# A graph network of GRU and attention layers on one core: more transposes through the DMA crossbar, and GpSimd broadcasts of f_j

## The chip, the core and the metric

The kernel runs on one core of one Trainium2 chip. The metric is the time of one execution on the device in microseconds, as the median of several runs. The core has TensorE (PE, matmuls and transposes, results to PSUM), ScalarE (ACT), VectorE (DVE), GpSimd (POOL) and SyncE (SP), which here only issues DMAs. Each engine takes its instructions in the order in which they were written and waits on semaphores for the others.

## The reference

There are 128 graphs of 128 nodes with 256 features, and an integer adjacency matrix for each. All is float32.

```python
# layer 0: three steps of a gated graph network
A = (adj != 0); h = x
for i in range(3):
    m = h @ weight[i]
    aggr = einsum('bst,bsd->btd', A, m)
    h = gru_cell(aggr, h, w_ih, w_hh, b_ih, b_hh)     # r, z: sigmoid; n: tanh
x = layernorm(x + h)
# layers 1 to 3: graph attention, each with its own W and a
Wh = x @ W.T
f_i, f_j = Wh @ a1, Wh @ a2
e = leaky_relu(f_i[:, :, None] + f_j[:, None, :], 0.2)
e = where(adj == 0, very_negative, e)
x = layernorm(x + softmax(e, axis=2) @ Wh)            # layer 2: rows without a neighbour give 0
```

## The kernel before

The 128 graphs are taken four at a time (`G = 4`), so there are 32 groups (`NG`). For each group `gru` (L516) does the three steps of layer 0 and `gat` (L648) the three attention layers.

In a step of `gru` the nodes' features are needed in two layouts. `hT` has the features on the partitions and four graphs of 128 nodes along the free dimension (two tiles for the 256 features, `KC = 2`). It feeds the gate products (L490), which `strassen` (L473) arranges as seven block products instead of eight, with sums and differences of blocks made by `sums` (L450, L460). `h` has the nodes on the partitions; it is the stationary operand of the aggregation by the mask `am` (L548). After steps one and two the new `hT2` has to be turned into `h`; after step three it has to be turned once more to be added to the input `y` (L635).

There are two ways to turn a tile. TensorE transposes four 128x128 blocks into a PSUM bank (L632 and others), and ScalarE or VectorE copies the bank out. `turned` (L375) goes through the DMA crossbar, which transposes 16-bit elements: one copy parts a float32 tile into its low and high halves (L382), SP issues the DMA transpose (L383), and a second copy joins the halves (L386). Before the change the crossbar is used for `x` of the groups from the third on and for `h` of steps one and two in all but the last four groups.

In a layer of `gat`, VectorE forms f_i and f_j as products with a row of `wa` and a sum (L660), one column for each graph. TensorE then transposes the column of f_j, broadcast along the free dimension, so that every partition gets the row of f_j in PSUM (L673, four transposes). VectorE adds the mask and takes the maximum (L678). ScalarE applies the leaky slope (L682) and the exponential with its sum (L699). TensorE transposes the scores (L706), which are copied out (for the first layer by `EVICT`; for the others with the scale of the previous layer norm, L711 or L715) and multiplied with the features (L736) and the weights (L747). VectorE adds the residual (L753); the sums of squares come from ScalarE (L434), epsilon from GpSimd (L438, and L418 in `layernorm`), and the power -0.5 from GpSimd (L406).

The order in which all this is issued is not written by hand. Every operation is given to a planner (`Plan`, L48) with the engines that may do it, a cost in ns for each, and the tiles that it reads and writes. `Plan.order` runs through time, gives each engine the ready operation with the lowest priority number, and emits the instructions in that order. An operation of TensorE counts as ready only `LATENCY` of the producer's engine and `MARGIN` after its last producer; a DMA has 4000 ns of latency on SP, to which an operation can add a `lag`. Operations marked `BOTH` or run on GpSimd share a port in the plan. Buffers are slots of a few kinds: `k2` (2 KB for each partition), `k4` (4 KB), `am`, PSUM banks `gate` and `bank`; a slot that is not free makes an operation wait in the plan. The priority of an operation comes from `stage` (L765): the number of its group, and for the last four groups (`LAST`) a number that takes them through their steps side by side. So the middle of the run is a steady state in which one group's attention is mixed with the GRU steps of the following ones, and the tail has four groups at once and nothing behind them.

Of the kernel before, what the change touches and what calls it, by code (L numbers as in the profile page):

```python
# [14 lines left out]
P = 128  # L15
# [32 lines left out]
class Plan:  # L48
# [6 lines left out]

    MARGIN = 300
# [8 lines left out]
    def op(self, engines, fn, reads=(), writes=(), prio=0, lag=0, port=("POOL",), start=0):  # L65
        o = Op(engines, fn, (prio[0], len(self.ops)), lag, port)
        o.group = prio[1]
        o.earliest = start
        norm = lambda k: k if isinstance(k, tuple) else (k, 0)
        for k in map(norm, reads):  # L70
            if k in self.writer:
                o.deps.add(self.writer[k])
            self.readers.setdefault(k, []).append(o)
            o.bufs.append(k[0])
        for k in map(norm, writes):
            if k in self.writer:
                o.deps.add(self.writer[k])
            o.deps.update(self.readers.pop(k, ()))
            self.writer[k] = o
            o.bufs.append(k[0])  # L80
        o.deps.discard(o)
        o.bufs = [b for b in dict.fromkeys(o.bufs) if b.tag]
        for b in o.bufs:
            b.left += 1
        self.ops.append(o)
# [113 lines left out]
def adj_resnorm_kernel(  # L199
# [24 lines left out]
    pools = {"gru": 5, "xs": 2, "adj": 2, "am": 4, "k2": 27, "k4": 18, "fx": 2, "jx": 2, "f": 4, "mv": 4, "st": 6, "v": 24,  # L224
             "gate": 4, "bank": 4}
    own = ({"k2": 6, "k4": 5, "gate": 1, "bank": 1, "v": 5, "fx": 0, "jx": 0, "st": 0}, {"k2": 3, "k4": 1, "bank": 1, "v": 5, "fx": 0, "jx": 0, "st": 0})
    floats = {"gru": 0, "k4": 1024, "xs": 1024, "fx": 256, "jx": 256, "f": 8, "mv": 8, "st": 6, "v": 4}
    tags = {t: (n, floats.get(t, 512)) for t, n in pools.items()}
    U16 = mybir.dt.uint16
    BOTH = ("DVE", "POOL")  # L230
    plan = Plan({t: n for t, (n, _) in tags.items()}, own)
    slots = {t: [(psum if t in ("gate", "bank") else work).tile([P, w], I32 if t == "adj" else F32, name=f"{t}{i}")
# [22 lines left out]


    ident = consts.tile([P, P], F32)
    make_identity(nc, ident)
# [35 lines left out]
    APART = {"ACT": 1000, "DVE": 620}  # L294
    TURN = 0
# [79 lines left out]
    def turned(src, key, dst, shape, prio):  # L375


        rows = Buf("k2", GN)
        flat = lambda: T(dst) if shape else T(dst).rearrange("p b q -> p (b q)")
        halves_of = lambda at: at.bitcast(U16).rearrange("p (h b q) -> p h b q", h=2, b=G)  # L380
        pairs_of = lambda at: at.bitcast(U16).rearrange("p b (q h) -> p h b q", h=2)
        plan.op(APART, lambda e: copy(e, halves_of(flat()), pairs_of(src())), reads=[key], writes=[dst], prio=prio, port=BOTH)  # L382
        plan.op({"SP": 1200}, lambda e: nc.sync.dma_start_transpose(  # L383
            T(rows).bitcast(U16).rearrange("p (a q) -> p a q", q=P), flat().bitcast(U16)),
            reads=[dst], writes=[rows], prio=prio, lag=TURN)
        plan.op(APART, lambda e: copy(e, pairs_of(T(dst).rearrange(shape, b=G) if shape else T(dst)), halves_of(T(rows))),  # L386
                reads=[rows], writes=[dst], prio=prio, port=BOTH)

# [21 lines left out]
    def layernorm(y, dst, prio):  # L410
# [7 lines left out]
        plan.op({"POOL": 229}, lambda e: nc.gpsimd.tensor_scalar(T(ve), T(mv)[:, :, 1], EPS, None, op0=ALU.add),  # L418
# [5 lines left out]
        for b in range(G):  # L424
            plan.op({"ACT": 500}, lambda e, b=b: nc.scalar.activation(  # L425
                T(dst)[:, b, :], T(y)[:, b, :], AF.Identity, bias=T(shift)[:, b:b + 1], scale=T(rstd)[:, b:b + 1]),
                reads=[(y, b), shift, rstd], writes=[(dst, b)], prio=prio)

    def deviation(y, before, prio):

        ss, ve = Buf("v", G), Buf("v", G)
        for b in range(G):
            jx = Buf("jx", D)
            plan.op({"ACT": 490}, lambda e, b=b, jx=jx: nc.scalar.activation(  # L434
                T(jx), T(y)[:, b, :], AF.Square, accum_out=T(ss)[:, b:b + 1]),
                reads=[(y, b)], writes=[jx, (ss, b)], prio=prio)
        if before is None:
            plan.op({"POOL": 229}, lambda e: nc.gpsimd.tensor_scalar(  # L438
# [77 lines left out]
    def gru(g, stage):  # L516

        xs, adj_i, am = Buf("xs", G, D), Buf("adj", G, P), Buf("am", G, P)
# [4 lines left out]
        plan.op({"SP": 60}, lambda e: nc.sync.dma_start(T(adj_i), adj[g * G:(g + 1) * G].rearrange("b s t -> s b t")),  # L523
                writes=[adj_i], prio=prio)
        if g == 0:
            input_weights(0, prio)
            hidden_weights(prio)
        plan.op({"DVE": 417}, lambda e: nc.vector.tensor_scalar(T(am), T(adj_i), 0, None, op0=ALU.not_equal),
                reads=[adj_i], writes=[am, turn], prio=prio, port=BOTH)
        if g < 2:  # L530
            hT = transposed(xs, lambda b, c: T(xs)[:, b, c * P:(c + 1) * P], prio)
        else:
            hT = [Buf("k2", GN) for c in range(KC)]
            for c in range(KC):
                turned(lambda c=c: T(xs)[:, :, c * P:(c + 1) * P], xs, hT[c], "p (b q) -> p b q", prio)
        h = None
        for i in range(STEPS):
            prio = stage(g, i)
            if g == 0 and i > 0:
                input_weights(i, prio)  # L540
# [76 lines left out]
            if last:  # L617
                y = Buf("k4", G, D)
                plan.op({"SP": 60}, lambda e: nc.sync.dma_start(T(y), x_g), reads=[agg[0]], writes=[y], prio=prio)
                plan.op({"DVE": 417}, lambda e: nc.vector.tensor_scalar(  # L620
# [3 lines left out]
            for c in range(KC):  # L624
                if not last and g < NG - LAST:
                    turned(lambda c=c, hT2=hT2: T(hT2[c]).rearrange("p (b q) -> p b q", b=G), hT2[c], h2[c], None, prio)
                    continue
# [20 lines left out]
    def gat(g, xc, no, stage):  # L648
# [3 lines left out]
        for l in range(3):  # L652
            prio = stage(g, STEPS + l)
            if g == 0:
                score_weights(l, prio)
            f = Buf("f", G, 2)
            for h in (1, 0):
                for b in range(G):
                    fx = Buf("fx", D)
                    plan.op({"DVE": 345}, lambda e, b=b, h=h, l=l, f=f, fx=fx, xc=xc: nc.vector.scalar_tensor_tensor(  # L660
                        T(fx), T(xc)[:, b, :], 1.0, T(wa)[:, l, h, :], op0=ALU.mult, op1=ALU.mult,
                        accum_out=T(f)[:, b, h:h + 1]), reads=[(xc, b), (wa, l)], writes=[fx, (f, 2 * b + h)], prio=prio, port=BOTH)
                if l:
                    plan.op({"DVE": 100}, lambda e, h=h, f=f, rstd=rstd: nc.vector.tensor_mul(
                        T(f)[:, :, h], T(f)[:, :, h], T(rstd)), reads=[(f, 2 * b + h) for b in range(G)] + [rstd],
# [3 lines left out]
            b_ = bank()  # L669

            def fn(e, b_=b_, f=f):
                for b in range(G):
                    nc.tensor.transpose(T(b_)[:, b * P:(b + 1) * P],  # L673
                                        T(f)[:, b, 1:2].to_broadcast([P, P]), ident)
            plan.op({"PE": 440}, fn, reads=[(f, 2 * b + 1) for b in range(G)], writes=[b_], prio=prio)

            for b in range(G):
                plan.op({"DVE": 215}, lambda e, b_=b_, b=b, e_=e_, top=top: nc.vector.tensor_tensor_reduce(  # L678
                    T(e_)[:, b, :], T(b_)[:, b * P:(b + 1) * P], T(no)[:, b, :], 1.0, 3 * FAR, ALU.add, ALU.max,
                    T(top)[:, b:b + 1]), reads=[b_, no], writes=[(e_, b), (top, b)], prio=prio)  # L680
            for b in range(G):
                plan.op({"ACT": 285}, lambda e, b=b, f=f, e_=e_: nc.scalar.activation(  # L682
                    T(e_)[:, b, :], T(e_)[:, b, :], AF.Prelu, bias=T(f)[:, b, 0:1], alpha=SLOPE),
                    reads=[(f, 2 * b), (e_, b)], writes=[(e_, b)], prio=prio)
            if l == 1:
# [6 lines left out]
                T(top), T(top), -1.0, T(f)[:, :, 0], op0=ALU.mult, op1=ALU.subtract),  # L692
# [9 lines left out]
            b_ = bank()  # L702

            def fn(e, b_=b_, e_=e_):
                for b in range(G):
                    nc.tensor.transpose(T(b_)[:, b * P:(b + 1) * P], T(e_)[:, b, :], ident)  # L706
            plan.op({"PE": 440}, fn, reads=[(e_, b) for b in range(G)], writes=[b_], prio=prio)
            if l:
                def scaled(e, b_=b_, pT=pT, rstd=rstd):
                    if e == "DVE":  # L710
                        nc.vector.tensor_mul(T(pT), T(b_).rearrange("p (b j) -> p b j", b=G),  # L711
                                             T(rstd).unsqueeze(2).to_broadcast([P, G, P]))
                    else:
                        for b in range(G):
                            nc.scalar.mul(T(pT)[:, b, :], T(b_)[:, b * P:(b + 1) * P], T(rstd)[:, b:b + 1])  # L715
                plan.op({"DVE": 630, "ACT": 1100}, scaled, reads=[b_, rstd], writes=[pT], prio=prio)
            else:
                plan.op(EVICT, lambda e, b_=b_, pT=pT: copy(e, T(pT).rearrange("p b j -> p (b j)"), T(b_)),
                        reads=[b_], writes=[pT], prio=prio)
# [45 lines left out]
    def stage(g, n):  # L765

        tail = NG - LAST
        return (g + (0 if n >= STEPS else 0) if g < tail else tail + n), 2 * g + (n >= STEPS)
# [5 lines left out]
    with tc.manual_schedule():  # L774
        for o in order:
# [43 lines left out]
```

## Time and profile before

| what | us |
|---|---|
| median of 3 runs | 2620.24 (2620.14 to 2620.81) |
| profiled execution, its own time | 2620.86 |
| its span, first to last instruction | 2618.9 |
| TensorE busy | 2578.3 |
| VectorE busy | 2084.6 |
| ScalarE busy | 1817.4 |
| GpSimd busy | 535.0 |
| 172 DMA transposes, each from issue to landing | 3.1 (median) |

"Busy" is the time in which at least one instruction of the engine has a record. Matmuls overlap each other on TensorE, so the mean of a group there is longer than the distance from one to the next; that distance is read from the chain of work that ended last, which lists pieces in order of time with their start and their length. In the sums by stage a line has the stretch, its length, then busy time and count for PE, PEld (weight loads), DVE, ACT and POOL, then the granted clock of TensorE, the share of the DMA engines and GB/s. In a line of groups the columns are: line, engine, operation, tiles out<-in with shapes, count, busy us and mean ns of one, and idle time before them with what ended it.

### The profile page before, as it was taken

The numbers are of one execution on the slowest core, as the hardware profiler recorded it, in microseconds if no ns is written. First come the engines' busy times: TensorE is split into PE (matmuls) and PEld (weight loads), VectorE is DVE, ScalarE is ACT, GpSimd is POOL, SyncE is SP. The second block draws the span as 40 slices with busy tenths as digits, with TensorE's granted clock in tenths as the row PEclk, the third lists the DMA queues.
The fourth block names the chain that finished last, engine by engine and source line by source line (L and its number), as shares of the span: only waits on it lengthen the run. The fifth ranks groups of instructions, "written<-read, shape, count | busy, mean of one in ns | idle before, by whom it ended". The sixth has DMA issues, their size and how long they took to land.

```text
span 2618.9 us, 41369 instructions
## 1 busy us (share of the span) xinstructions
PE 2578.3 (98%) x13848; PEld 2297.8 (88%) x13848; DVE 2084.6 (80%) x6162; ACT 1817.4 (69%) x4572; POOL 535.0 (20%) x602
## 2 busy tenths in 40 slices
PE   8999999999999999999999999999999999999988
PEld 7888888888889988888888889888889888888877
DVE  6688878888888888788888888888888878856787
ACT  5677666767777767777777777777777777654566
POOL 2122221212122222122212122212122212211111
PEclk9999999999999999999999999999999999999999
DMA  5211111212112111112211121211122221000000
GB/s 146 52 29 37 47 51 25 53 45 48 36 39 53 45 45 42 36 45 53 45 45 41 33 49 45 53 45 41 33 49 45 50 48 37 21 9 25 9 1 33
DMA packets 251734, 110.43 MB, mean 42 GB/s; under 512 B 184320, under 2 KB 249856, under 8 KB 251520
## 3 DMA queue, kind: packets, MB, share of 16 engines
q1 hardware_dynamic: 251088, 107.77, 17.2%
q8 instruction: 109, 1.79, 0.3%
q14 instruction: 105, 0.86, 0.1%
q10 hardware_dynamic: 432, 0.01, 0.0%
HBM read 45.89 MB, written 16.78 MB: 24 GB/s over the span
## 4 chain that ended last, share of the span: by engine, by line
PE 92%; DVE 6%; ACT 1%; issue 1%; DMA 0%; POOLq 0%; SPq 0%; ACTq 0%; DVEq 0%
PE gate L490 64%; PE bank L747 11%; PE bank L736 6%; PE bank L548 6%; DVE fx L660 1%; PE bank L706 1%; PE bank L673 1%; PE bank L632 1%; DVE k L753 1%; PE bank L341 1%; DVE k L290 1%; DVE k L495 0%; DVE k L610 0%; DVE k L678 0%; DVE k L590 0%
## 5 line engine op out<-in xcount | busy, mean ns | idle before, releaser
L490 PE MATMUL gate<-k,whs 128*128 128x256 f32 x4032 | 1202.8, 380 | 2.6 <-DVE k L495 1.8
L490 PE MATMUL gate<-k,wcs 128*128 128x256 f32 x4032 | 1201.0, 379 | 0.0
L490 PEld LDWEIGHTS gate<-k,wcs 128*128 128x128 f32 x4032 | 767.3, 190 | 104.5
L490 PEld LDWEIGHTS gate<-k,whs 128*128 128x128 f32 x4032 | 734.9, 191 | 88.5 <-DVE k L495 2.5
L495 DVE TENSOR_TENSOR k<-gate,k 128x512 f32<-128x512 f32 x576 | 391.9, 685 | 204.0 <-PE gate L490 143.6
L747 PE MATMUL bank<-gwT,k 128*128 128x256 f32 x1536 | 348.9, 380 | 0.4 <-DVE k L290 0.2
L460 POOL TENSOR_TENSOR k<-k,k 128x256 f32<-128x256 f32 x251 | 214.5, 862 | 557.0 <-DVE k L460 236.3
L747 PEld LDWEIGHTS bank<-gwT,k 128*128 128x128 f32 x1536 | 288.7, 190 | 41.2 <-DVE k L290 2.4
L574 ACT ACTIVATE k<-k,brz 128x256 f32<-128x256 f32 (+1 forms) x384 | 225.1, 621 | 134.8 <-DVE k L495 134.8
L660 DVE SCALAR_TENSOR_TENSOR fx<-k,wa 128x256 f32<-128x256 f32 x768 | 285.6, 424 | 16.4 <-ACT k L425 16.3
L288 ACT COPY k<-k 128x1024 uint16<-128x1024 uint16 x203 | 257.7, 1290 | 10.8 <-DVE k L613 7.8
L288 ACT COPY k<-bank 128x512 f32<-128x512 f32 (+1 forms) x307 | 177.2, 581 | 115.7 <-PE bank L736 48.0
L434 ACT ACTIVATE jx<-k 128x256 f32<-128x256 f32 x384 | 156.0, 407 | 133.8 <-DVE k L753 133.1
L556 ACT COPY k<-gate 128x512 f32<-128x512 f32 x288 | 166.9, 581 | 88.7 <-PE gate L490 88.2
L406 POOL TENSOR_TENSOR v<-v,neghalf 128x4 f32<-128x4 f32 x128 | 134.6, 1051 | 375.8 <-DVE v L445 353.1
L753 DVE SCALAR_TENSOR_TENSOR k<-bank,v,k 128x256 f32<-128x256 f32 x384 | 166.7, 474 | 40.4 <-PE bank L747 40.2
L736 PEld LDWEIGHTS bank<-k,k 128*128 128x128 f32 x1536 | 189.5, 195 | 8.8 <-DVE k L290 1.6
L736 PE MATMUL bank<-k,k 128*128 128x128 f32 x1536 | 190.5, 278 | 3.0 <-DVE k L290 1.2
L699 ACT ACTIVATE k<-k,v 128x128 f32<-128x128 f32 x384 | 149.3, 390 | 61.4 <-DVE v L695 61.3
L603 ACT ACTIVATE k<-k,bi 128x512 f32<-128x512 f32 x192 | 137.6, 718 | 70.7 <-DVE k L600 47.1
L610 DVE SCALAR_TENSOR_TENSOR k<-k,k 128x512 f32<-128x512 f32 x192 | 143.4, 748 | 40.9 <-POOL k L608 39.9
L560 ACT ACTIVATE k<-gate,bhn 128x256 f32<-128x256 f32 x288 | 135.9, 472 | 50.7 <-PE gate L490 47.2
(90 smaller groups left out, 2995.6 us busy)
## 6 DMA issues: line engine op xcount, KB each, us to landing
xs<-in_x_dram SPq DMA_DIRECT2D x32, 512.0 KB, 3.8
k<-in_x_dram SPq DMA_DIRECT2D x32, 512.0 KB, 3.9
out_dram<-k SPq DMA_DIRECT2D x32, 512.0 KB, 2.9
adj<-in_adj_dram SPq DMA_DIRECT2D x32, 256.0 KB, 2.8
k<-k SPq DMA_TRANSPOSE x172, 3.1
k<-in_gnn_wT_dram SPq DMA_DIRECT2D x3, 256.0 KB, 4.8
k<-in_w_ihT_dram SPq DMA_DIRECT2D x2, 384.0 KB, 5.6
k<-in_w_hhT_dram SPq DMA_DIRECT2D x2, 384.0 KB, 6.0
```

The costliest lines, as they stand in the source:

```text
L288: nc.scalar.copy(dst, src)
L434: plan.op({"ACT": 490}, lambda e, b=b, jx=jx: nc.scalar.activation(T(jx), T(y)[:, b, :], AF.Square, accum_out=T(ss)[:, b:b + 1]), reads=[( ...
L460: nc.vector if e == "DVE" else nc.gpsimd).tensor_tensor(T(t)[:, j, :], a(), b(), ALU.subtract),
L490: nc.tensor.matmul(T(dst)[:, j * H:(j + 1) * H], T(w)[:, m, gt, :], moving(m, ms)[1](), start=first and n == 0, stop=n == len(todo) - 1, s ...
L495: plan.op({"DVE": 630}, lambda e: nc.vector.tensor_add(T(o)[:, :, j * H:(j + 1) * H], T(b_).rearrange("p (g n) -> p g n", g=2), T(part).re ...
L548: nc.tensor.matmul(T(b_)[:, b * P:(b + 1) * P], src, T(am)[:, b, :], start=True, stop=True)
L556: plan.op({"ACT": 500}, lambda e: nc.scalar.copy(T(dst), T(src)), reads=[src], writes=[(dst, 0), (dst, 1)], prio=prio)
L574: nc.scalar.activation(T(o)[:, gt, n0:n1], src(), AF.Tanh, bias=brz[:, gt * KC + c:gt * KC + c + 1], scale=0.5)
L660: plan.op({"DVE": 345}, lambda e, b=b, h=h, l=l, f=f, fx=fx, xc=xc: nc.vector.scalar_tensor_tensor(T(fx), T(xc)[:, b, :], 1.0, T(wa)[:, l, ...
L736: nc.tensor.matmul(T(b_)[:, b * P:(b + 1) * P], T(xc)[:, b, c * P:(c + 1) * P], T(pT)[:, b, :], start=True, stop=True)
L747: nc.tensor.matmul(T(b_)[:, (b - b0) * D:(b - b0 + 1) * D], T(aT[k])[:, b * P:(b + 1) * P], T(gwT)[:, l, k, :], start=(k == 0), stop=(k == ...
L753: nc.vector.scalar_tensor_tensor(T(y)[:, b, :], T(b_)[:, (b - b0) * D:(b - b0 + 1) * D], T(rden)[:, b:b + 1], T(xc)[:, b, :], op0=ALU.mult ...
```

## The change

- In all groups but the last four, `h` of the third step goes through `turned` and is then added to `y` from SBUF, and so do the scores of the first attention layer.
- In the same groups f_j is spread by GpSimd. `f` is now a tile of 128x128 with the f_j of graph b in column 32b. One TensorE transpose puts the four rows on partitions 0, 32, 64 and 96 of PSUM, a copy brings them to SBUF (`row`), and four partition broadcasts write them to the score tile, to which VectorE then adds the mask in place. A GpSimd library that has the broadcast is loaded at the start, and the standard one again after the last of them.
- The adjacency is loaded into the slot of `am` and turned into the mask in place; the separate `adj` buffers are gone.
- Epsilon is added by VectorE instead of GpSimd (L418, L438).
- The results that nobody reads (`fx`, `jx`) go to two shared tiles.
- The planner gets other costs for the copies around the crossbar (`APART`, `TOGETHER`), a lag of -1800 ns for the transposes (`TURN`), other numbers of slots, and priorities by stage (`LATER`). On ScalarE the joining copy walks the elements in another order.

```diff
-    pools = {"gru": 5, "xs": 2, "adj": 2, "am": 4, "k2": 27, "k4": 18, "fx": 2, "jx": 2, "f": 4, "mv": 4, "st": 6, "v": 24,
-             "gate": 4, "bank": 4}
+    pools = {"gru": 5, "xs": 2, "am": 5, "k2": 29, "k4": 18, "f": 4, "mv": 4, "st": 6, "v": 24,
+             "gate": 5, "bank": 3}
+    LATER = (-0.25, 1.5, -0.25, 0, 0, 1.5)
...
-    APART = {"ACT": 1000, "DVE": 620}
-    TURN = 0
+    APART = {"ACT": 960, "DVE": 615}
+    TOGETHER = {"ACT": 1340, "DVE": 615}
+    TURN = -1800
...
-    def turned(src, key, dst, shape, prio):
+    def turned(src, keys, dst, prio):
...
+        def together(e):
+            if e == "ACT":
+                nc.scalar.copy(flat().bitcast(U16).rearrange("p (q h) -> p q h", h=2),
+                               T(rows).bitcast(U16).rearrange("p (h q) -> p q h", h=2))
+            else:
+                copy(e, flat().bitcast(U16).rearrange("p (q h) -> p h q", h=2),
+                     T(rows).bitcast(U16).rearrange("p (h q) -> p h q", h=2))
...
-        plan.op(APART, lambda e: copy(e, pairs_of(T(dst).rearrange(shape, b=G) if shape else T(dst)), halves_of(T(rows))),
-                reads=[rows], writes=[dst], prio=prio, port=BOTH)
+        plan.op(TOGETHER, together, reads=[rows], writes=[dst], prio=prio, port=BOTH)
...
-        plan.op({"POOL": 229}, lambda e: nc.gpsimd.tensor_scalar(T(ve), T(mv)[:, :, 1], EPS, None, op0=ALU.add),
+        plan.op({"DVE": 100}, lambda e: nc.vector.tensor_scalar(T(ve), T(mv)[:, :, 1], EPS, None, op0=ALU.add),
...
+        plan.op({"SP": 60}, lambda e: nc.sync.dma_start(T(am).bitcast(I32), adj[g * G:(g + 1) * G].rearrange("b s t -> s b t")),
+                writes=[am], prio=prio)
+        plan.op({"DVE": 340}, lambda e: nc.vector.tensor_scalar(T(am), T(am).bitcast(I32), 0, None, op0=ALU.not_equal),
+                reads=[am], writes=[am, turn], prio=prio, port=BOTH)
...
+                if last and g < NG - LAST:
+                    hx = Buf("k2", G, P)
+                    turned(lambda c=c, hT2=hT2: T(hT2[c]).rearrange("p (b q) -> p b q", b=G), [hT2[c]], hx, prio)
+                    plan.op({"DVE": 620}, lambda e, hx=hx, c=c, y=y: nc.vector.tensor_add(
+                        T(y)[:, :, c * P:(c + 1) * P], T(hx), T(y)[:, :, c * P:(c + 1) * P]), reads=[hx, turn, (y, 0)],
+                        writes=[(y, b) for b in range(G)], prio=prio, port=BOTH)
+                    continue
...
-            f = Buf("f", G, 2)
+            f = Buf("f", G, P // G)
...
+            if g < NG - LAST:
+                plan.op({"PE": 115}, lambda e, b_=b_, f=f: nc.tensor.transpose(
+                    T(b_)[:, 0:P], T(f).rearrange("p b h -> p (b h)"), ident),
+                    reads=[(f, 2 * b + 1) for b in range(G)], writes=[b_], prio=prio)
+                row = Buf("k2", P)
+                plan.op({"ACT": 250, "DVE": 200}, lambda e, b_=b_, row=row: copy(e, T(row), T(b_)[:, 0:P]),
+                        reads=[b_], writes=[row], prio=prio)
+                for b in range(G):
+                    plan.op({"POOL": 300}, lambda e, row=row, b=b, e_=e_: nc.gpsimd.partition_broadcast(
+                        T(e_)[:, b, :], T(row)[b * P // G:b * P // G + 1, 0:P]), reads=[row], writes=[(e_, b)], prio=prio)
+                if g == NG - LAST - 1 and l == 2:
+                    plan.op({"POOL": 7000}, lambda e: nc.gpsimd.load_library(library_config.standard),
+                            reads=[(e_, b) for b in range(G)], writes=[Buf(None)], prio=prio)
...
+            by_xbar = g < NG - LAST and l == 0
+            if by_xbar:
+                turned(lambda e_=e_: T(e_), [(e_, b) for b in range(G)], pT, prio)
+            else:
...
-        return (g + (0 if n >= STEPS else 0) if g < tail else tail + n), 2 * g + (n >= STEPS)
+        return g + LATER[n] if g < tail else tail + n, 2 * g + (n >= STEPS)
...
+        make_identity(nc, ident)
+        nc.gpsimd.load_library(library_config.all_libraries[10])
```

## The prediction

> **What bounds the kernel now.** I read the shares of the span first, then the chain that ended last, then that chain piece by piece in the middle of the run, then the waits of TensorE, then the sums by stage.
>
> ```profile
> PE 2578.3 (98%) x13848; PEld 2297.8 (88%) x13848; DVE 2084.6 (80%) x6162; ACT 1817.4 (69%) x4572; POOL 535.0 (20%) x602
> ...
> PE 92%; DVE 6%; ACT 1%; issue 1%; DMA 0%; POOLq 0%; SPq 0%; ACTq 0%; DVEq 0%
> PE gate L490 64%; PE bank L747 11%; PE bank L736 6%; PE bank L548 6%; DVE fx L660 1%; PE bank L706 1%; PE bank L673 1%; PE bank L632 1%; DVE k L753 1%; PE bank L341 1%; DVE k L290 1%; DVE k L495 0%; DVE k L610 0%; DVE k L678 0%; DVE k L590 0%
> ```
>
> TensorE is busy for 98% of the span and is 92% of the chain. The chain has the three lines that the change cuts down: L632 (h of a step), L673 (f_j) and L706 (scores), 1% each. The pieces of the chain from 1000 to 1080 us give their price:
>
> ```profile
> 1008.89 0.44 PE bank L632 x4
> 1009.33 8.64 PE gate L490 x40
> 1017.96 0.44 PE bank L673 x4
> 1018.40 6.05 PE gate L490 x28
> 1024.45 0.44 PE bank L706 x4
> 1024.88 0.89 PE bank L548 x8
> ```
>
> Each piece starts where the one before it ends: no gap at all. Four transposes take 0.44 us, so 0.11 us each. The sums by stage say where this holds (PE busy is the second number):
>
> ```profile
> 0.00:20.00 20.00, 12.48 (x46) 9.37 (x47) 9.31 (x20) 8.40 (x14) 5.32 (x12) 0.91 0.69 225
> 20.00:140.00 120.00, 120.00 (x594) 103.91 (x594) 84.21 (x168) 73.20 (x128) 15.27 (x16) 1.00 0.29 70
> 140.00:2200.00 2060.00, 2054.01 (x11104) 1837.77 (x11103) 1679.20 (x4953) 1481.10 (x3711) 445.84 (x503) 1.00 0.19 44
> 2200.00:2619.00 419.00, 391.84 (x2109) 346.71 (x2107) 311.90 (x1023) 254.72 (x721) 68.60 (x71) 0.97 0.06 18
> ```
>
> TensorE idles 7.5 us at the start, 6.0 us in the 2060 us of the middle and 27.2 us in the tail. A group takes 78.98 us (1000.26 to 1079.24 in the chain), all of it TensorE's. So in the middle a microsecond taken off TensorE is a microsecond of time, while the other engines keep up.
>
> **What the Trainium skill says.** "Perfetto Trace Analysis", Identifying the Most-Contended Engine: matmul busy time is a bad metric because matmuls are pipelined. "TensorE: Matmul & The Clock Gate", Part 4, has about 275 ns for a transpose in a kernel's context. The trace shows both: the record of a transpose lasts 273 ns (L632), but four take 0.44 us in the chain. The 0.11 us is the price; 273 ns would claim 2.5 times too much. "SBUF — State Buffer", Who interferes with whom: a VectorE instruction with two SBUF inputs contends with a GpSimd instruction that reads SBUF. The trace agrees: a GpSimd subtraction (L460) is 0.73 us in many pieces of the timeline and 862 ns in the mean. "GPSIMD Engine Reference", Instruction dispatch: the first call after loading a library pays about 6 us; no row of before shows one.
>
> **The change part by part.** Counts are from the written order of both kernels.
>
> TensorE, removed. Groups 0 to 27 lose 8 transposes for h of the third step, 4 for the scores of the first layer, and 9 of 12 for f_j (one transpose of a 128x128 tile now yields the rows of all four batches). That is 21 x 28 = 588 (L632 320 to 96, L706 384 to 272, f_j 384 to 84 + 48). 588 x 0.110 us = **64.7 us**, 2.31 us a group. All other products keep their counts. A group's floor falls from 78.98 to 76.67 us.
>
> ScalarE. An h or score tile goes through the crossbar in three moves: a copy that parts 16-bit halves, the DMA, a copy that joins them. 84 tiles more (172 to 256). Partings on ScalarE go from 74 to 154: 80 x 1.04 us (the row of xs) = +83. Joinings 164 to 191: 27 x 1.34 (median of the k copies, 1000 to 1200 us) = +36. Evictions of 128x512 302 to 214: 88 x 0.58 = -51. New copies of the 128x128 row, 44 at about 0.3 (128x256 is 0.37) = +13. Sum +81: 1898 us, 74% of the new span.
>
> VectorE. Partings and joinings 106 to 167: 61 x 0.70 = +43. Evictions 140 to 200: 60 x 0.68 = +41. Row copies 40 x 0.3 = +12. The sums moved from GpSimd (L418, L438), 64 x 0.165 = +11. Subtractions of L460 449 to 379: 70 x 0.46 = -32. Sum +75: 2160 us, 84%. A group has 67 us of VectorE work in 76.7; it stays behind TensorE, by less than before.
>
> GpSimd. 336 partition broadcasts; the trace has none. Nearest row of the groups: the 128x128 select at the start, the last line here.
>
> ```profile
> L406 POOL TENSOR_TENSOR v<-v,neghalf 128x4 f32<-128x4 f32 x128 | 134.6, 1051 | 375.8 <-DVE v L445 353.1 <-DVE v L720 6.1 <-DVE f L664 5.8
> ...
> masks.py:199 POOL TENSOR_SCALAR_AFFINE_SELECT ident<-ident 128x128 f32<-128x128 f32 x1 | 0.3, 292 | 0.1
> ```
>
> (The first line is the upper bound: 1.05 us, for an operation of few elements.) I take 0.3 us, as the kernel's plan does; its other GpSimd costs (1035, 1250, 720, 229) were measured as 1051, 1276, 862 and 258 to 355, so a plan figure is not far off. 336 x 0.3 = +101, L460 +70 x 0.86 = +60, L608 -5, L418 and L438 -20: 671 us, 26%. Hidden beside TensorE unless the four in a row are long (rival below). Bounds on the path: 0, or the loss worked out there. A gain is excluded.
>
> Library loads. The first stands after the identity, done at 1.3 us; GpSimd's next work was at 6.85 us, and TensorE starts at 12.3 us and first does 16 records of L341 (6.55 us). A load of 6 us delays the sums to some 8 to 10 us: hidden; the upper bound is 6 us. The second stands in group 27, with products of groups 28 to 31 queued on TensorE; behind it on GpSimd wait pow and L608 of those groups. 0 to 6 us; I take 0.
>
> Crossbar and SP. 84 x 1.24 us more of issue on SP: per group 9 x 1.24 = 11 us and four loads and stores under 0.6 each, in 76.7. The queue's 17.2% of the DMA engines becomes at most 17.2 x 256/172 = 26%. Latency: the transposes land 3.0/3.1/4.9 us (min/median/max) after issue. The plan before counted 1.2 + 4.0 = 5.2 us until the joining copy, the new one (TURN -1800) 3.4 us. So the median transpose still lands in time, but the latest is 1.5 us late, and the copy waits at the head of ScalarE's or VectorE's queue, with evictions behind it and TensorE behind those. The plan holds TensorE back 0.5 us after either engine (MARGIN 300 and LATENCY 200 to 220), so 1.0 us of such a case arrives. Before, all waits of copies for the crossbar were 6.4 us (5 cases). I charge 4 such cases: **+4 us**. Bounds: 0 to 30 (126 pairs at a quarter of 1 us).
>
> At nothing: the adjacency turned into its mask in place (same 32 operations; an adjacency load now waits for one of five am slots, with transposes queued behind it on SP, where it already waited 259.9 us for L528 unharmed), shared scratch tiles, 5 gate and 3 bank slots (21 banks a group less are asked for), earlier weights. Bounds of these together: 5 us either way.
>
> Moved: LATER puts step 1 and the third layer 1.5 groups later. In the written order TensorE has 165 us of work left after group 27's last product, before 245 (432, 222 and 110 ns each, which the chain confirms): more to fill the tail with. I take 0; up to -11 of the 27.2 us.
>
> Sum: 2620.86 - 64.7 + 4 = 2560.2 us against the profiled execution (span 2618.9 and 2.0 around it). That stands 0.6 above the median 2620.24, so the forecast is **2560 us**.
>
> **The rivals.**
> A, the forecast: 55%, 2552 to 2570.
> B, half eaten: VectorE at 88% of a group and late transposes leave gaps on TensorE, some 1 us a group: 2556 + 29 = 2585. For: little reserve, a shorter allowance. Against: no gap at 82% now. 20%.
> C, more: the tail is filled too, 2556 - 11 = 2545. For: 27.2 us idle there. Against: its last 100 us hold only groups 28 to 31, unchanged. 13%.
> D, slower: the broadcasts. Four stand one after another between the transpose of f_j and the masked sum, 84 times. At 1.05 us each they end 4 x 0.75 = 3.0 us late; the plan's margin for GpSimd (0.25 + 0.3) covers 0.55; 2.45 x 84 = 206 us: 2762. Slower from 64.7/84 = 0.77 us a layer, that is from 0.3 + (0.77 + 0.55)/4 = 0.63 us a broadcast. For: no row shows one. Against: the select's 292 ns. 9%.
> E, the change does not do what it says on the path: TensorE's removed work comes back as waits, 2616 to 2625. Against: the counts. 3%.
>
> **How the numbers follow.** A measurement of this kernel can tell about 0.2% (5 us) from no change. Faster is A, B and C: 0.88; the same E, 0.03; slower D, 0.09. The range 2543 to 2598 holds A, nearly all of C and most of B; D, E and the tail of B stay outside.
>
> **What would show it.** Right: 6890 products in the order give a TensorE chain without gaps at 76.7 us a group, three lines shrunk in the chain, VectorE near 84%, a broadcast near 0.3 us, hardly any wait of TensorE for a joining copy. Wrong: a period above 77.5 us; TensorE's waits led by the copies after the crossbar (B) or by the masked sum behind GpSimd (D).

## The result, and the profile after

The changed kernel takes **2658.28 us** (median of 4 runs, 2655.33 to 2660.45), the kernel before 2620.52 (2620.14 to 2621.12, 4 runs): ratio 1.0143, 95% interval 1.0126 to 1.0161. The forecast was 2560 with 88% for faster. It is slower by 38 us and 98 us off. The profiled execution took 2658.43 us, span 2656.7.

The page of the kernel after: busy shares, then the chain of work that ended last by engine and by line.

```profile
PE 2542.6 (96%) x13260; PEld 2233.9 (84%) x13260; DVE 2231.3 (84%) x6328; ACT 1873.7 (71%) x4626; POOL 700.4 (26%) x940
...
PE 64%; DVE 25%; ACT 5%; DMA 3%; issue 3%; POOL 1%; DVEq 0%; POOLq 0%; ACTq 0%; SPq 0%
PE gate L506 46%; PE bank L790 7%; DVE nobody L682 7%; PE bank L779 5%; PE bank L564 3%; DVE k L299 3%; DVE k L796 2%; DVE k L511 2%; DMA k<-k 2%; DVE k L476 1%; DVE k L606 1%; DVE k L717 1%; ACT k L442 1%; ACT k L738 1%; DMA xs<-in_x_dram 1%
```

The 588 matmuls are gone (13848 to 13260). But TensorE is 64% of the chain instead of 92%, and VectorE a quarter of it, led by L682, the products that form f_i and f_j. (Lines moved with the edit: the gates L490 are L506 now, the f products L660 are L682, f_j's transpose L673 is L694 in the groups of the steady state and L711 in the last four, the masked sum L678 is L717, the product with the scores L736 is L779, the aggregation L548 is L564, the subtractions L460 and L608 are L476 and L624.)

The sums by stage of the kernel after, columns as before:

```profile
0.00:20.00 20.00, 12.24 (x53) 9.49 (x54) 9.43 (x27) 8.13 (x15) 4.89 (x12) 1.00 0.80 250
20.00:140.00 120.00, 118.23 (x585) 101.07 (x584) 79.48 (x153) 70.72 (x128) 18.60 (x22) 1.00 0.30 71
140.00:2200.00 2060.00, 1982.06 (x10314) 1744.44 (x10313) 1784.11 (x4990) 1490.92 (x3637) 578.26 (x787) 1.00 0.24 52
2200.00:2657.00 457.00, 430.06 (x2314) 378.87 (x2312) 358.27 (x1163) 303.92 (x849) 98.64 (x120) 0.99 0.10 26
```

Start and tail are as before (7.8 and 26.9 us of idle TensorE). The middle is not: 77.9 us idle in 2060, where there were 6.0. A group takes 81.8 us there (24 transposes of L694, eight groups, lie 654.4 us apart), not 76.7.

TensorE's waits after: line, what it waited for, us in total, times, longest.

```profile
PE bank L694 <- DVE nobody L682: 36.4, 38, 2.3
PE bank L779 <- DVE k L299: 12.9, 8, 2.4
PE bank L694 <- DVE f L686: 11.2, 6, 3.6
PE gate L506 <- ACT k L579: 7.4, 8, 1.2
...
PE bank L779 <- ACT k L395: 4.3, 6, 2.1
PE gate L506 <- DVE k L511: 4.0, 9, 0.9
```

f_j comes late from VectorE, and the scores come late through the crossbar (L299 and L395 are the joining copies). Gaps under 0.16 us don't show here, since matmul records overlap. So I also took every piece of TensorE's timeline and subtracted, from the distance to the next piece's start, 0.216 us for each 128x256 product and 0.11 for each 128x128 one (0.43 for the few of 128x512). What is over, put down to the line that starts late, I call **TensorE's gaps**. They sum to 52 us before and 154 after; the 103 more are the miss (2658.4 against 2620.9 - 64.7 = 2556.2, 102). By line, after against before: f_j's transposes 60.9 (56.2 at L694, 4.7 at L711) against 5.3, the product with the scores 27.6 against 5.0, the gates 44.6 against 13.2.

### The profile page after: what moved, and what is told of

The parts are those of the page before. It is cut to its first block, busy times and chain, and to the rows that moved or that the text cites. A ratio compares the mean times of both kernels' runs of the same rounds, so it can differ in the third digit from the quotient of the medians.

```text
span 2656.7 us, 41132 instructions
## 1 busy us (share of the span) xinstructions
PE 2542.6 (96%) x13260; PEld 2233.9 (84%) x13260; DVE 2231.3 (84%) x6328; ACT 1873.7 (71%) x4626; POOL 700.4 (26%) x940
## 4 chain that ended last, share of the span: by engine, by line
PE 64%; DVE 25%; ACT 5%; DMA 3%; issue 3%; POOL 1%; DVEq 0%; POOLq 0%; ACTq 0%; SPq 0%
PE gate L506 46%; PE bank L790 7%; DVE nobody L682 7%; PE bank L779 5%; PE bank L564 3%; DVE k L299 3%; DVE k L796 2%; DVE k L511 2%; DMA k<-k 2%; DVE k L476 1%; DVE k L606 1%; DVE k L717 1%; ACT k L442 1%; ACT k L738 1%; DMA xs<-in_x_dram 1%
## 5 line engine op out<-in xcount | busy, mean ns | idle before, releaser
L506 PE MATMUL gate<-k,whs 128*128 128x256 f32 x4032 | 1209.7, 382 | 15.5 <-ACT k L579 7.4
L506 PE MATMUL gate<-k,wcs 128*128 128x256 f32 x4032 | 1202.6, 380 | 0.0
L506 PEld LDWEIGHTS gate<-k,wcs 128*128 128x128 f32 x4032 | 768.8, 191 | 105.3
L506 PEld LDWEIGHTS gate<-k,whs 128*128 128x128 f32 x4032 | 743.2, 191 | 119.7 <-ACT k L579 11.0
L682 DVE SCALAR_TENSOR_TENSOR nobody<-k,wa 128x256 f32<-128x256 f32 x768 | 350.3, 456 | 39.1 <-PE bank L694 8.9
L423 POOL TENSOR_TENSOR v<-v,neghalf 128x4 f32<-128x4 f32 x128 | 144.7, 1131 | 856.4 <-DVE v L461 449.0
L476 POOL TENSOR_TENSOR k<-k,k 128x256 f32<-128x256 f32 x280 | 232.2, 843 | 284.5 <-DVE k L476 85.4
L450 ACT ACTIVATE nobody<-k 128x256 f32<-128x256 f32 x384 | 159.4, 415 | 147.7 <-DVE k L796 138.4
L395 ACT COPY k<-k 128x1024 uint16<-128x1024 uint16 x191 | 221.7, 1163 | 41.8 <-DMA k<-k 40.3
L297 ACT COPY k<-bank 128x512 f32<-128x512 f32 (+2 forms) x263 | 137.2, 527 | 147.8 <-PE bank L779 51.4
L779 PEld LDWEIGHTS bank<-k,k 128*128 128x128 f32 x1536 | 188.0, 195 | 34.6 <-DVE k L299 11.6
L779 PE MATMUL bank<-k,k 128*128 128x128 f32 x1536 | 194.0, 280 | 22.9 <-DVE k L299 12.9
L624 POOL TENSOR_TENSOR k<-k,k 128x512 f32<-128x512 f32 x81 | 107.0, 1322 | 338.1 <-ACT k L619 294.4
L701 POOL PARTITION_BROADCAST k<-k x336 | 128.6, 483 | 213.0 <-ACT k L297 99.8
L299 DVE COPY k<-bank 128x512 f32<-128x512 f32 (+1 forms) x241 | 147.2, 617 | 29.1 <-PE bank L779 10.9
```

The lines of the kernel that those rows point to most:

```text
L299: nc.vector.tensor_copy(dst, src)
L395: nc.scalar.copy(flat().bitcast(U16).rearrange("p (q h) -> p q h", h=2), T(rows).bitcast(U16).rearrange("p (h q) -> p q h", h=2))
L450: plan.op({"ACT": 415}, lambda e, b=b: nc.scalar.activation(nobody[0], T(y)[:, b, :], AF.Square, accum_out=T(ss)[:, b:b + 1]), reads=[(y, ...
L476: nc.vector if e == "DVE" else nc.gpsimd).tensor_tensor(T(t)[:, j, :], a(), b(), ALU.subtract),
L506: nc.tensor.matmul(T(dst)[:, j * H:(j + 1) * H], T(w)[:, m, gt, :], moving(m, ms)[1](), start=first and n == 0, stop=n == len(todo) - 1, s ...
L682: plan.op({"DVE": 345}, lambda e, b=b, h=h, l=l, f=f, xc=xc: nc.vector.scalar_tensor_tensor(nobody[1], T(xc)[:, b, :], 1.0, T(wa)[:, l, h, ...
```

## The experiments

The theory from this profile (S): each f product now writes the same scratch tile as the one before it, and so waits for the own engine's last write; likewise the squares on ScalarE. Rivals: the crossbar's shorter allowance (T), contention of VectorE with GpSimd (G), late scores (X), copies of the third step (B).

VectorE's timeline, first before, then after (start, length, engine, line, operation):

```profile
1035.40 0.41 DVE L660 SCALAR_TENSOR_TENSOR fx<-k,wa 128x256 f32<-128x256 f32 x1
1035.74 0.08 DVE L660 DVE_READ_ACCUMULATOR fx<-k,wa 128x1 f32 x1
1035.74 0.42 DVE L660 SCALAR_TENSOR_TENSOR fx<-k,wa 128x256 f32<-128x256 f32 x1
```

```profile
1082.27 0.42 DVE L682 SCALAR_TENSOR_TENSOR nobody<-k,wa 128x256 f32<-128x256 f32 x1
1082.61 0.09 DVE L682 DVE_READ_ACCUMULATOR nobody<-k,wa 128x1 f32 x1
1082.73 0.42 DVE L682 SCALAR_TENSOR_TENSOR nobody<-k,wa 128x256 f32<-128x256 f32 x1
```

Before, the next product starts with the accumulator's read; after, 0.12 us behind it. The records hardly grow (0.42 us, median) and no idle time is listed; the distance of starts shows the wait, 0.35 us before and 0.47 after. These are medians of products that directly follow another one, 489 of the 768 in the kernel after. ScalarE's squares have 0.42 and 0.54 (226 of 384 after).

**e1: two scratch halves.** The tiles are viewed as 16-bit, the halves alternate, and the written order stays the same on every engine.

```diff
-    nobody = [consts.tile([P, D], F32, name=f"nobody{i}") for i in range(2)]
+    nobody = [consts.tile([P, D], F32, name=f"nobody{i}").bitcast(mybir.dt.bfloat16) for i in range(2)]
...
-                nobody[0], T(y)[:, b, :], AF.Square, accum_out=T(ss)[:, b:b + 1]),
+                nobody[0][:, b % 2 * D:(b % 2 + 1) * D], T(y)[:, b, :], AF.Square, accum_out=T(ss)[:, b:b + 1]),
...
-                        nobody[1], T(xc)[:, b, :], 1.0, T(wa)[:, l, h, :], op0=ALU.mult, op1=ALU.mult,
+                        nobody[1][:, b % 2 * D:(b % 2 + 1) * D], T(xc)[:, b, :], 1.0, T(wa)[:, l, h, :], op0=ALU.mult, op1=ALU.mult,
```

> The changed kernel, same order on all engines, but the two shared scratch tiles are read as bf16 and each has two halves, used in turn, so that no product of L682 (VectorE) and no square of L450 (ScalarE) writes where the one just before it wrote. Theory S (scratch: each of these waits for the write of the one before, 0.12 us each on VectorE and 0.13 on ScalarE, so VectorE comes late with f_j and TensorE stops at L694): starts of neighbouring products go from 0.47 back to 0.35 us, waits of TensorE at L694 fall from 47.6 to under 15 us, and the time falls to 2575 to 2610 us. Rival T (crossbar allowance of the plan too short, TURN): about 2650. Rival G (VectorE and GpSimd in each other's way since the broadcasts): about 2640.

Measured: **2612.59 us**, ratio to before 0.997 (0.9958 to 0.9983). Distances are back at 0.35 and 0.42 us. TensorE's waits at L694 fall from 47.6 to 18.6 us, not under 15, and the time lies 3 us above the range: S is a cause, but not the only one. VectorE's busy time falls too, from 2231.3 to 2196.2 us: the records of neighbours overlap again (above, 0.42 us long at a distance of 0.35), and with one tile they don't.

**e2: the control.** The same 16-bit view, always the same half (`b % 2` becomes 0).

> Control for the one above: scratch tiles read as bf16, but always the same half. All theories: as the changed kernel, 2650 to 2665 us; if it is faster, the type of the scratch matters and not the waiting.

Measured: 2660.32 us, ratio 1.0148 (1.0133 to 1.0163); distance 0.47. The narrower output saves nothing; the second place does.

**e3: the reverse in the kernel before.** Both slots of `fx`, and of `jx`, are laid on one tile; the order stays.

```diff
+    [slots[t].__setitem__(1, slots[t][0]) for t in ("fx", "jx")]
```

> The kernel before, same order on all engines, with its two fx slots and its two jx slots laid on one tile each. Theory S: starts of neighbouring products of L660 go from 0.35 to 0.47 us, VectorE has 20% idle to take it, but waits appear on TensorE: 2630 to 2670 us. Rivals T and G: within 3 us of 2620.

Measured: 2642.85 us, ratio 1.0082 (1.0067 to 1.0097); distances 0.47 and 0.54. The same wait costs 23 us there (557 products directly behind another one) and 46 us in the changed kernel (489): its price is not one of the count alone, which fits VectorE's smaller reserve.

**e4: a longer allowance.** `TURN = 0` in the changed kernel.

> The changed kernel with TURN = 0, so that the plan counts 5.2 us for a crossbar transpose as the kernel before did. Theory S: 2640 to 2670 us, waits at L694 stay. Rival T: 2560 to 2600 us. Rival G: as S.

Measured: 2740.91 us, ratio 1.0458 (1.0442 to 1.0473), with gaps of 240 us: outside the range of every theory. The planner's own total tells most of it: 2663 us with 0, 2563 with -1800 (2607 for the kernel before). T as the main cause falls: with the longer allowance the span still stands 79 us above its plan, with the shorter one 94.

With the scratch tile mended, 52 us to the forecast are open. e1's gaps are 108 us, 57 more than before: 23 more at f_j's transposes (24.9 at L694), 22 more at the product with the scores (27.4 at L779), 21 more at the gates (33.8), and some 9 less elsewhere. The expectations below leave the gates out; they give 25.6 for the 27.4 and, in e9, 20 for 22.7, because products at the edges of the stretches read counted twice there. Four runs on the base of e1 follow. e5, e6 and e7 undo one part each and are planned anew, so their differences hold the new order too.

**e5: the scores by TensorE again** (`by_xbar = False`).

> The changed kernel with two halves of the scratch tiles (2612.6 us), and the scores of the first layer turned by TensorE again in all groups: 112 transposes more, 112 x 0.11 = 12.3 us of TensorE. If this part only saves TensorE's work: 2625. If the crossbar's scores are what comes late (theory X; TensorE waited 13.2 + 4.4 us at L779 for joining copies): the 18 us go, 2595 to 2607, or lower if the copies' queues had held up more behind them.

Measured: 2604.58 us, ratio 0.9934 (0.9919 to 0.9949), the value of theory X. The gap at L779 falls from 27.4 to 7.3 us. So this part of the change loses 8 us: its waits cost more than the 12.3 us of TensorE that it saves. One wait in e1 shows how (SP's issues, then VectorE's joining copy):

```profile
1524.57 0.37 SPq L538 DMA_DIRECT2D xs<-in_x_dram  x1
1525.04 6.05 SPq L401 DMA_TRANSPOSE k<-k  x3
```

```profile
1529.65 0.74 DVE L299 COPY k<-k 128x1024 uint16<-128x1024 uint16 x1 [1.71 <-DMA k<-k]
```

The parting copy ended at 1523.9, but a load of x stood ahead on SP and was issued until 1524.9; then the first of the three transposes needed 4.6 us instead of its usual 3.1. The plan had 3.4 us for all of it.

**e6: f_j by TensorE again** (the branch with the broadcasts is not taken).

> The same base (2612.6 us), f_j turned and spread by TensorE as before, no broadcast: 252 transposes more, 27.7 us of TensorE. If the broadcasts cost nothing beside it: 2640. Theory G, in which the broadcasts and the masked sum with two SBUF inputs slow VectorE and GpSimd (some 383 sums at 0.38 in place of 0.22 us, and 336 broadcasts on GpSimd, 52 us open in all): at most 2612, down to 2590 if it is the whole cause.

Measured: 2644.64 us, ratio 1.0086 (1.007 to 1.0103): 32 us worse than e1, where 27.7 are TensorE's and 4 lie in the first 20 us (TensorE 8.64 us busy, in e1 12.61). The broadcasts and the sums behind them cost nothing net. G falls in this form.

**e7: h of the third step by TensorE again.**

> The same base (2612.6 us), h of the third step turned by TensorE as before: 224 transposes more, 24.6 us of TensorE. If this part saves only TensorE's work: 2637. If the parting and joining copies load VectorE and ScalarE to the point that TensorE waits for them (rival B of the prediction): 2600 to 2615.

Measured: 2642.46 us, ratio 1.0077 (1.0062 to 1.0092): 30 us worse than e1 for 24.6 us of TensorE. This part gives all that was computed; B falls in this form.

**e8: a memset in place of each broadcast.** The order is e1's.

```diff
-                    plan.op({"POOL": 300}, lambda e, row=row, b=b, e_=e_: nc.gpsimd.partition_broadcast(
-                        T(e_)[:, b, :], T(row)[b * P // G:b * P // G + 1, 0:P]), reads=[row], writes=[(e_, b)], prio=prio)
+                    plan.op({"POOL": 300}, lambda e, row=row, b=b, e_=e_: nc.gpsimd.memset(
+                        T(e_)[:, b, :], 0.0), reads=[row], writes=[(e_, b)], prio=prio)
```

> The same base (2612.6 us) in the same written order, with a GpSimd memset of the same 128x128 tile in place of each partition broadcast: f_j is left out of the scores. If the broadcasts' duration (0.43 us) or their reading of SBUF beside VectorE costs the open 52 us (theory G): 2575 to 2600. If not: within 5 us of 2612.

Measured: 2605.14 us, ratio 0.9935 (0.992 to 0.995). 7.5 us, hardly more than the other theory's 5, and far from 2575 to 2600. The broadcasts are not the main cause.

What else holds VectorE? In e1, VectorE and then GpSimd in the same stretch:

```profile
1294.43 0.41 DVE L682 SCALAR_TENSOR_TENSOR nobody<-k,wa 128x256 bf16<-128x256 f32 x1
1294.77 0.08 DVE L682 DVE_READ_ACCUMULATOR nobody<-k,wa 128x1 f32 x1
1294.77 1.48 DVE L682 SCALAR_TENSOR_TENSOR nobody<-k,wa 128x256 bf16<-128x256 f32 x1
1296.18 0.08 DVE L682 DVE_READ_ACCUMULATOR nobody<-k,wa 128x1 f32 x1
```

```profile
1294.56 1.41 POOL L624 TENSOR_TENSOR k<-k,k 128x512 f32<-128x512 f32 x1 [7.73 <-ACT k L619]
```

The first product takes 0.34 us to its accumulator's read. The second meets a subtraction that GpSimd began 0.21 us before, and takes 1.41. The Trainium skill's "SBUF — State Buffer", Who interferes with whom, has the rule: a VectorE instruction with two SBUF inputs contends with a GpSimd instruction that reads SBUF, not with one that only writes it. The trace agrees: in e1 the product takes 0.503 us in the mean beside GpSimd work and 0.345 alone (159 and 609 cases). L717, whose second input was in PSUM before, now has two inputs in SBUF in all but the last four groups: 0.359 and 0.211 (179 and 205 cases), where before both were 0.21.

**e9: GpSimd only writes.** e1's order; where GpSimd had a subtraction, it has a memset of the result (VectorE's stay).

```diff
-                nc.vector if e == "DVE" else nc.gpsimd).tensor_tensor(T(t)[:, j, :], a(), b(), ALU.subtract),
+                nc.vector.tensor_tensor(T(t)[:, j, :], a(), b(), ALU.subtract) if e == "DVE" else nc.gpsimd.memset(T(t)[:, j, :], 0.0)),
...
-                    nc.vector if e == "DVE" else nc.gpsimd).tensor_tensor(T(d), T(h_), T(v)[:, 0, :], ALU.subtract),
+                    nc.vector.tensor_tensor(T(d), T(h_), T(v)[:, 0, :], ALU.subtract) if e == "DVE" else nc.gpsimd.memset(T(d), 0.0)),
```

> The changed kernel with two halves of the scratch tiles (2612.6 us), in the same written order, with a memset of the result in place of each subtraction that GpSimd has at L476 and L624; these subtractions are left out of the result. In the trace of the base a VectorE product at L682 lasts 0.34 us alone and up to 1.4 us while GpSimd subtracts. If these stalls of VectorE are why TensorE waits at L694 (24.9 us) and L779 (25.6 us): both fall to under 10 us each, 2570 to 2590. If the waits come from the order and the crossbar's landing alone: 2605 to 2615.

Measured: **2571.47 us**, ratio 0.9812 (0.9798 to 0.9827), 41 us better than e1. The groups of VectorE after (line, operation, count, busy us, mean ns), the rows of the accumulators left out, and TensorE's waits:

```profile
L682 DVE SCALAR_TENSOR_TENSOR nobody<-k,wa 128x256 bf16<-128x256 f32 x768 | 291.7, 420 | 27.3 <-PE bank L694 18.8 <-ACT k L442 5.9
L717 DVE CUSTOM_DVE_ANT_0 k<-k,am 128x128 f32<-128x128 f32 x336 | 83.6, 290 | 3.8 <-POOL k L701 3.5
```

```profile
PE bank L779 <- DVE k L299: 10.2, 8, 2.3
...
PE bank L779 <- ACT k L395: 4.2, 6, 1.8
PE bank L694 <- DVE nobody L682: 3.1, 8, 0.8
...
PE bank L694 <- DVE f L686: 1.8, 2, 1.1
```

In the kernel after the same two rows have 456 and 363 ns. Beside GpSimd or alone, the product now takes 0.347 and 0.345 us, the sum 0.219 and 0.211. VectorE's busy time falls from 2196.2 us in e1 to 2073.3, with the same instructions: 123 us were spent in GpSimd's way. The gaps shrink by 41 us: 16.7 at L694 (24.9 to 8.2), 16.8 at the gates, but only 4.7 at L779 (27.4 to 22.7), against what I had written.

The memsets are also shorter than the subtractions (372 ns against 834 at L476, 572 against 1309 at L624), so what reads their results can start earlier. VectorE's waits for GpSimd's subtractions tell how much that can be, first in the kernel before, then in e1:

```profile
DVE k L610 <- POOL k L608: 39.9, 44, 1.3
```

```profile
DVE k L626 <- POOL k L624: 3.2, 3, 1.2
DVE k L476 <- POOL k L476: 2.1, 1, 2.1
```

In e1 they are 5.3 us, so by these waits earlier results explain little of the 41.

**e10, e11, e12: the planner's figures.** e11 tells the planner that f_j is ready 600 ns later (`lag=600` on L682 and L686). e12 gives the scores' transposes -600 in place of -1800. e10 has the scores by TensorE and f_j 400 ns later.

> A candidate for the best version: two halves of the scratch tiles, the scores of the first layer by TensorE (2604.6 us), and the planner told that f_j is ready 400 ns later. The planner's own time is 2564 us against 2573 for the kernel without the 400 ns, which measured 28 to 31 us more than its plan. If the plan's error at L694 (27 us of waits) is what is left: 2575 to 2590. If the waits only move: 2592 to 2605.

> All parts of the change, two halves of the scratch tiles, and the planner told that f_j is ready 600 ns later. Its own time is 2575 us; the base's is 2563 and measured 2612.6, 50 more. If the lateness at L694 (24.9 us) is one half of what is open: 2575 + 50 - 20 = 2605 and hardly a wait at L694. If the waits only move to other lines: 2615 to 2630.

> All parts of the change, two halves of the scratch tiles, and an allowance of -600 in place of -1800 ns for the crossbar transposes of the scores alone. The planner's own time is 2581 us. If the lateness of these transposes at L779 (25.6 us) is the other half: 2581 + 50 - 20 = 2611 and hardly a wait at L779: the plan loses as much as the waits gain. If VectorE's lateness is behind both: L779 keeps 10 us or more, 2615 to 2630.

Measured: **2597.58** (ratio 0.9912, 0.9897 to 0.9926), 2602.41 (0.9927, 0.9911 to 0.9944) and 2624.49 us (1.0016, 1.0009 to 1.0023). Of the kernels without memsets e10 is the fastest, and it beats both the kernel before and the one after; its gap at L694 is still 21.1 us, so the waits mostly moved. e11 keeps all parts of the change: L694 falls to 13.3 us, and L564 has 22.4 instead of 6.0; as its time says, the first theory held, though not clean. e12 keeps 17.8 us at L779 and has 48.3 at the gates instead of 33.8: the second theory. A later date for one product moves VectorE's lateness to the next.

**e13 and e14: the controls of e9.** The memsets in the kernel before (e13), and in the changed kernel with its one scratch tile (e14).

> The control of e9: the kernel before, in its own order, with a memset of the result in place of each subtraction that GpSimd has at L460 and L608; these subtractions are left out of the result. If GpSimd's hold on VectorE was there before but hidden behind TensorE (the theory): 2610 to 2621. If lighter GpSimd work speeds any of these kernels up, whatever the change: 2575 to 2590, and then the 41 us of e9 don't belong to the change.

> The changed kernel (one scratch tile, 2658.3 us) with the same memsets in place of GpSimd's subtractions, which are left out of the result. If the wait for the own write (46 us) and GpSimd's hold on VectorE (41 us) add: 2617. If they are one lack of reserve on VectorE, of which each relief makes good the same part: 2575 to 2600.

Measured: 2611.70 us (0.9962, 0.9947 to 0.9977) and 2605.70 us (0.994, 0.9923 to 0.9956). In the kernel before the memsets give 10 us, in the changed one 53 with one scratch tile and 41 with two. VectorE's busy time falls by 78 us in the kernel before (2084.6 to 2006.3, the page of e13), where hardly any of it was on the path:

```profile
PE 2574.1 (99%) x13848; PEld 2298.9 (88%) x13848; DVE 2006.3 (77%) x6162; ACT 1817.0 (70%) x4572; POOL 284.2 (11%) x602
```

The 10 us of the kernel before need not be contention: its 39.9 us of waits for L608 (shown at e9) are gone in e13.

e14 fits neither theory alone: scratch tile and contention give 87 us together (2658.3 to 2571.5); one by one 46 and 53 make 99. So 12 us are common, the rest adds.

**e15: the sums by VectorE.** e1, with L476 no longer offered to GpSimd (`{"DVE": 350}`).

> A candidate that computes everything: the change with two halves of the scratch tiles (2612.6 us), and the sums of L476 no longer offered to GpSimd, so that VectorE has all of them (389 more at 0.34 us in place of GpSimd's 0.83). The planner's own time is 2561 us, the base's 2563. If GpSimd's SBUF subtractions cost more on VectorE than the same work costs there: 2575 to 2598. If VectorE's load is what counts, whoever causes it (2196 us busy, +132 of own work): 2612 to 2650.

Measured: 2619.27 us, ratio 1.0 (0.9991 to 1.0009). The second theory held, VectorE's load counts, whoever causes it: it is busy for 2220.3 us, and the gap at L694 is 46.9.

**e16: the scores by TensorE, on e9.**

> The closing of the account: two halves of the scratch tiles, the scores of the first layer by TensorE, and memsets in place of GpSimd's subtractions, which are left out of the result. e9 (2571.5 us) still had 20 us of waits at L779; TensorE has 12.3 us more work. If the late scores are the last of the three causes: 2571.5 - 20 + 12.3 = 2564, with under 5 us at L779. If L779 was VectorE's lateness in another place: 2575 to 2584.

Measured: 2570.99 us, ratio 0.9812 (0.9798 to 0.9827). The gap at L779 falls from 22.7 to 7.8 us (4.6 of them listed as waits), close to what the first theory said, but the time stays, 7 us above it: what the waits give back (14.9 us) and what TensorE pays (12.3) nearly cancel, and the other lines add the rest. Crossbar scores gain nothing even with VectorE unhindered.

## Why the prediction was wrong

**TensorE, removed: right.** 588 transposes at 0.11 us. Put back, 224 cost 30 us (e7) and 252 cost 28 without the start (e6), 24.6 and 27.7 computed.

**The step that failed: "At nothing: ... shared scratch tiles", with "5 us either way".** It named no cover, and there was none. Two rotating tiles became one, and each f product that directly follows another one (489 of 768) then starts 0.12 us later, behind the write before it. That is some 59 us of VectorE's time, of which 35 show in its busy sum (2196.2 to 2231.3), and 46 us of the run (e1). The diff showed the edit and the written order showed the wait of VectorE on itself; no row of before could show its price, so it needed a bound of 768 waits of unknown length, not a place among the free ones. Rival B came nearest (VectorE's reserve eaten, gaps at TensorE), but it was sized at 29 us from late transposes.

**VectorE: mis-sized.** The sum said 2160 us, 84%; measured were 2231.3. 35 of the 71 us more are the scratch tile's (2196.2 in e1). For the rest, the copies were counted, but not what GpSimd does to VectorE. The prediction cited the rule of contention and used it for GpSimd's 0.86 us alone. The changed sum's move from one SBUF input to two is in the diff ("adds the mask in place"), and costs 0.08 us in each of 336 cases, 26 us of VectorE (361 ns in e1, 283 before); GpSimd held VectorE for 78 us before and 123 in e1.

**Busy share was the wrong measure of reserve.** 84% looked like cover. But TensorE, in order, waits for f_j 84 times at a date that the plan fixed with 0.5 us of slack. The planner's own totals, 2607 us before and 2563 after, gained 44 us; measured spans stood 12 us above the plan before and 94 after (e1: 48; e9: 7).

**Crossbar: right mechanism, undersized.** 4 us were charged (bounds 0 to 30). The joining copies waited 58 us (6.4 before), and TensorE 17 us for them at L779; for the scores alone, e9 and e16 put the cost, ahead of the 12.3 us that TensorE saves, at some 13 us, e1 and e5 at 20. The landings had their median of 3.1 us and a maximum of 5.9, not 4.9.

**GpSimd: 671 us forecast, 700.4 measured.** A broadcast lasts 0.43 us (median) and follows the one before after about 0.3, half of rival D's threshold of 0.63. D's sign was right, its cause not: the broadcasts alone give 7.5 us (e8). **ScalarE** was forecast at 1898 us, measured 1873.7. **Start and tail.** The prediction has TensorE start at 12.3 us; in the trace of before it starts at 5.06 (L397) and only goes on at 12.29 after a pause. Nothing hung on it: GpSimd's first subtraction comes at 9.12 us, within the 8 to 10 that were said (6.85 before), and the idle time of the start stays. The tail kept its 26.9 us; with the scratch tile mended it fell to 18.3 (e1), 9 less than before. That this is rival C's 11 us, from the new priorities, was not tested.

**The account.** Forecast to measured 98 us: 46 for the scratch tile (e1), 31 for GpSimd's subtractions (e9's 41 less the 10 that they cost the kernel before too, e13), and 21 left. Taken in the other order the first two are 34 and 43 (e14): their sum of 77 is measured, their split depends on the order. For the 21, e9's gap at L779 is 17.7 us above that of before (22.7 against 5.0). This term is an agreement of size: e16 took 14.9 of these away and got back only 12.8 (0.5 of time and TensorE's 12.3), so some 8 us stay open.

## What to carry to other kernels

A scratch output that nobody reads still needs two places in turn: with one, an instruction right behind another waits for its own engine's last write. No idle time was listed for it here, and the busy sum showed 35 of some 59 us; only the distance between starts shows it whole. Before an engine's spare share is used as cover, ask what dates it has to keep, and what each moved operand does to its neighbours: an input that goes from PSUM to SBUF brings a VectorE instruction into GpSimd's way. A fixed order turns the lateness of an engine with time to spare into waits of the one that has none, and later dates in the plan only move them.

## What was not expected of the hardware

- A wait of an engine for its own last write costs 0.12 us on VectorE (0.47 against 0.35 from start to start, 128x256) and nearly 0.13 on ScalarE (0.54 against 0.42). The Trainium skill's "VectorE: DVE Perf Modes", The DRAIN you can't avoid, measured that a semaphore after each of eight copies costs nothing extra; here, where the next product waits on it, it costs a third of the product.
- One product of 0.34 us lasted 1.41 us to its accumulator's read, which came 0.21 us after the end of GpSimd's subtraction: VectorE stood for nearly the whole of it.
